# Two cross-attention layers on one core: image scores of layer 2 read from the row maxima's scores, and another order inside its slots

## The chip, the core and the metric

The kernel runs on one core of a Trainium2 chip. The metric is the device time of one execution in microseconds (us). A core has five engines that run side by side, each with its own order of instructions: TensorE (PE in the profile; PEld is its loading of weights, which overlaps the matmuls), VectorE (DVE), ScalarE (ACT), GpSimd (POOL) and SyncE (SP), which here only issues DMAs. ScalarE issues a few DMAs too. They wait for each other through semaphores.

## The reference

Sixteen sequences of 256 rows and 320 channels go through two cross-attention layers with 20 heads of 16. Each has a context of 256 tokens of 512 numbers, the last four of which are image tokens. Layer 2 is (cut to what matters):

```python
text_ehs = encoder_hidden_states[:, :-NUM_TOKENS]
ip_ehs = encoder_hidden_states[:, -NUM_TOKENS:]
q = heads(hidden_states @ W_q)
k_t, v_t = heads(text_ehs @ W_k), heads(text_ehs @ W_v)
probs_t = softmax(einsum('bhsd,bhtd->bhst', q, k_t) * attn_scale)
text_out = einsum('bhst,bhtd->bhsd', probs_t, v_t)
k_ip, v_ip = heads(ip_ehs @ W_k_ip), heads(ip_ehs @ W_v_ip)
attn_scores = einsum('bhsd,bhnd->bhsn', q, k_ip) * attn_scale
qsem = l2norm(einsum('bhst,bte->bhse', probs_t, text_ehs))
sem = einsum('bhse,bne->bhsn', qsem, l2norm(ip_ehs))
probs_ip = softmax(attn_scores + SEM_SCALE * sem) * spatial_mask
ip_out = einsum('bhsn,bhnd->bhsd', probs_ip, v_ip)
out = (text_out + ip_out) @ W_out + b_out + residual
```

`attn_scores`, the **image scores**, are 4 numbers per row and head. The **norm** of `qsem` is worked out as a square root of a form in the probabilities, not from `qsem` itself. Layer 1 differs in its semantic term and is not touched but at its last step.

## The kernel before

The work is cut into **slots**. A slot is one group of 4 heads of one batch: 16 batches of 5 groups make 80 slots a layer (NS = 80, NG = 5). Slots k = 0 to 79 are layer 1 (`slot0`), k = 80 to 159 are layer 2 (`slot1`); one or two more finish the pipeline. TensorE's order is written out by hand and pinned; in the main loop the other engines' orders are made by a scheduler. Between the parts of a slot stand points (0.33, 0.67, 1.0) at which `fill` runs every prepared step that is due by then: projections, keys, values, images, each a generator in `tasks` with due times counted in slots (L1046ff).

A layer-2 slot k has these parts. The 256 columns of a product are two halves (0 and 1).

- **T**, the scores with text rows on the partitions (L798), and **exps** of them on ScalarE (L811), which give `P[k]`. T reads rows XROW to KS1 of the stacked queries, which hold the row maxima. They are matmuls of 50 rows, two at a time in the array.
- **S**, the scores of group k+2 with query rows on the partitions (L803, 48 rows). VectorE reduces them to row maxima (L804) over the text columns [:T1]; columns T1 to S are those of the four image tokens.
- **attend1**: for group k-2 the values (L848), 32-column matmuls of `P`, and the ones' product `zone` (L851) over `W`; settled by VectorE and POOL (`settle1`: transpose L893, POOL copy L894, reciprocal L896, product L897).
- **rounded1** for group k: ScalarE rounds half of P (L829), POOL takes P minus that (L830), which gives `R` and `W`.
- **norm1** for group k-1: full 128-row matmuls of R (L839), four for n = 0 and three for n = 1, for both halves u of the group; VectorE multiplies them into `W` (L840). In the text, norm00, norm01, norm10 and norm11 are norm1(k-1, u, n).
- **maxima1** for group k+2: two small matmuls turn the maxima (L817), ScalarE copies them (L819) and issues two DMAs into rows of the stacked queries (L821).
- **stacks1** for group k+4: SyncE loads queries and keys (L648).

`both1(k, t)` issues T, S, the reduce, then what stands `between` (attend1), then the exps. The order is both1(k, 0) with attend1 between, norm00, fill 0.33, norm01, both1(k, 1), rounded 0, stacks, norm10, fill 0.67, norm11, rounded 1, maxima(k+2), fill 1.0.

Image work: `open1` projects the queries (`queries`), makes `kb` of the image keys with `image1` (two VectorE products of 128x384 with a constant mask, L529), multiplies it with the queries in nine matmuls (`prod`, L205) and transposes the product to `si` (L978). `image_softmax` (L904 to L946) takes the norms' parts `norms[b]` (`nt`, six numbers per row, head: index 0 the sum, 1 to 4 the semantic products, 5 the squared form), and `si`; `close1` multiplies with the image values (L954), projects and stores.

Other lines that the prediction names: L147 and L148 split context and keys into two parts (a cast on ScalarE, a difference on VectorE or POOL); L476 makes `tph`, a scaled copy of the context, on ScalarE; L541 is a difference of a split; L551 projects queries and output; L421 is a copy in the preparation. PSUM has banks for T, P (attend), X (all else) and S (BANKS).

Of the kernel before, what the change touches and what calls it, by code (L numbers as in the profile page):

```python
# [16 lines left out]
B = 16  # L17
S = 256
# [30 lines left out]
def xattn2(  # L49
# [47 lines left out]
    words, slots = {"ctb": 1024, "cta": 1024, "raw": 512, "rawc": 512, "kb": 1152, "si": 256, "sp": 128, "wC": 2 * 4 * (H * D + NIP), "mt": S, "mx": 2, "kst": 4 * S, "rs": 2 * S, "P": 4 * S}, {}  # L97
# [189 lines left out]
    kmask = const_tile([128, 3, 32], "kmask")  # L287
# [83 lines left out]
    def weights1():  # L371
# [3 lines left out]
        dma(cipn, cip_d)  # L375
        yield
# [33 lines left out]
    def weights6():  # L410
# [15 lines left out]
        dma(kmask, kmask_d.rearrange("(m p) c -> p m c", p=128))  # L426
# [97 lines left out]

    def image1(b):

        kb = buf("kb", [128, 2, 3, 32, NIP], FR)
        for s in range(2):
            nc.vector.tensor_mul(  # L529
                kb[:, s],  # L530
                f(kip[:, s, :, 4 * b : 4 * b + 4]).unsqueeze(2).to_broadcast([128, 3, 32, NIP]),
                kmask.unsqueeze(3).to_broadcast([128, 3, 32, NIP]),
            )
        return kb.rearrange("p s m c n -> p s m (c n)")
# [116 lines left out]
    def stacks1(k):  # L651
# [5 lines left out]
        qd = get("o1", b)[0]  # L657
# [126 lines left out]
    def both1(k, t, between=None):  # L784
# [7 lines left out]
        if c:  # L792
            st = [bank("T").rearrange("p (h t) -> p h t", h=2) for u in range(2)]
            lo = (0, DUP)[t]
            for j in range(2):
                for u in range(2):
                    rows = slice(64 * u, 64 * u + KS1)
                    mm(st[u][:, j], c[1][rows, j, lo : lo + 128], c[0][rows, j], start=True, stop=True)  # L798
        if a:
            for j in range(2):  # L800
                for u in range(2):
                    rows = slice(64 * u, 64 * u + XROW)
                    mm(sp[:, 2 * u + j], a[0][rows, j, t * 128 : (t + 1) * 128], a[1][rows, j], start=True, stop=True)  # L803
            anchor(nc.vector.tensor_reduce(maxes[k + 2][:, t], sp[:, :, :T1], axis=AX.X, op=ALU.max))  # L804
        if between:
            between()
# [35 lines left out]
    def attend1(k):  # L842
        b, g = divmod(k - NS, NG)
        v, pv = get("t1", b)[0], bank("P")
        for n in range(2):
            for s in range(4):
                h = V1W * (4 * g + s)
                mm(pv[32 * s : 32 * s + 32, :S], v[:, n, h : h + 32], P[k, s % 2][:, n, s // 2], start=n == 0, stop=False)  # L848
        for n in range(2):
            for s in range(4):  # L850
# [357 lines left out]
```

## Time and profile before

| | |
|---|---|
| median of 3 runs | 1620.4 us (1616.49 to 1623.62) |
| the profiled execution | 1612.52 us |
| its span in the profile | 1610.7 us, mean granted clock 0.977 |
| TensorE busy, of the span | 1518.9 us, 94%, 13194 matmuls |
| VectorE busy | 1212.2 us, 75% |
| ScalarE busy | 847.1 us, 53% |
| GpSimd busy | 1195.7 us, 74% |

The views answer: the page gives each engine's busy time and forty slices of the span (digits are tenths; PEclk is the clock that TensorE was granted). The windows give the same by stretches of 100 us. The groups give, by line and engine, count, busy time, mean duration in ns and the idle time just before with what ended it. The timeline gives single instructions, or runs of like ones, with their start. A matmul's duration contains the pipeline's tail, so the next one starts earlier than it ends.

### The profile page before, as it was taken

The numbers are of one execution on the slowest core, as the hardware profiler recorded it, in microseconds if no ns is written. First come the engines' busy times: TensorE is split into PE (matmuls) and PEld (weight loads), VectorE is DVE, ScalarE is ACT, GpSimd is POOL, SyncE is SP. The second block draws the span as 40 slices with busy tenths as digits, with TensorE's granted clock in tenths as the row PEclk, the third lists the DMA queues.
The fourth block names the chain that finished last, engine by engine and source line by source line (L and its number), as shares of the span: only waits on it lengthen the run. The fifth ranks groups of instructions, "written<-read, shape, count | busy, mean of one in ns | idle before, by whom it ended". The sixth has DMA issues, their size and how long they took to land.

```text
span 1610.7 us, 36262 instructions
## 1 busy us (share of the span) xinstructions
PE 1518.9 (94%) x13194; PEld 1218.1 (76%) x13194; DVE 1212.2 (75%) x2426; ACT 847.1 (53%) x1861; POOL 1195.7 (74%) x1227
## 2 busy tenths in 40 slices
PE   7899999999999899789999999999999999999996
PEld 6787878787878787577777777777777777777765
DVE  5466777777777678877877787778777887788785
ACT  5344545555555545446656556555655655565562
POOL 3358787878787867777688768876877787778785
PEclk9899999999999899799999999999999999999998
DMA  6767777777677576665424333433343333423301
GB/s 218 214 200 204 206 204 206 205 205 211 199 204 210 170 213 174 162 198 177 149 67 133 114 127 96 131 119 120 96 136 121 107 109 127 130 90 104 110 27 45
DMA packets 235741, 243.05 MB, mean 151 GB/s; under 512 B 19050, under 2 KB 219468, under 8 KB 235564
## 3 DMA queue, kind: packets, MB, share of 16 engines
q1 hardware_dynamic: 233356, 239.44, 49.7%
q8 instruction: 105, 1.72, 0.4%
q10 hardware_dynamic: 2208, 1.30, 0.3%
q14 instruction: 72, 0.59, 0.1%
HBM read 116.78 MB, written 88.18 MB: 127 GB/s over the span
## 4 chain that ended last, share of the span: by engine, by line
PE 63%; DMA 9%; DVE 8%; POOL 8%; ACT 4%; issue 3%; SPq 1%; ACTq 0%; POOLq 0%; DVEq 0%
PE X L205 16%; PE X L839 13%; PE X L551 7%; PE P L732 6%; PE P L848 4%; PE S L675 4%; PE T L798 3%; PE P L851 3%; PE T L699 3%; POOL wt L830 2%; DMA kd<-kst 2%; DMA qs<-qd 2%; DMA qs<-mt 2%; PE S L803 2%; DVE wt L840 1%
## 5 line engine op out<-in xcount | busy, mean ns | idle before, releaser
L705 POOL TENSOR_TENSOR P<-P,rs 128x512 f32<-128x512 f32 x320 | 413.8, 1313 | 149.6 <-ACT P L702 149.5
L830 POOL TENSOR_TENSOR wt<-P,ctb 128x512 f32<-128x512 f32 x320 | 419.0, 1324 | 95.0 <-ACT ctb L829 93.6
L839 PE MATMUL X<-ctb,gm 128*128 128x512 f32 x1120 | 329.9, 412 | 0.7 <-DVE wt L840 0.4
L702 ACT ACTIVATE P<-T 128x512 f32<-128x512 f32 x320 | 176.0, 595 | 211.8 <-PE T L699 113.9
L839 PEld LDWEIGHTS X<-ctb,gm 128*128 128x128 f32 x1120 | 188.9, 188 | 69.2 <-issue 15.2
L840 DVE TENSOR_TENSOR wt<-X,wt 128x512 f32<-128x512 f32 x320 | 218.4, 683 | 18.9 <-PE X L839 13.4
L804 DVE TENSOR_REDUCE mn<-S 128x4 fp32r<-128x1008 f32 x160 | 191.7, 1198 | 49.1 <-PE S L803 48.9
L829 ACT ACTIVATE ctb<-P 128x512 fp32r<-128x512 f32 x320 | 195.1, 630 | 40.1 <-PE X L839 35.8
L811 ACT ACTIVATE P<-T 128x512 f32<-128x512 f32 x320 | 173.1, 593 | 68.9 <-PE P L848 53.8
L677 DVE TENSOR_REDUCE mn<-S 128x4 fp32r<-128x716 f32 x160 | 142.5, 891 | 0.0
L699 PE MATMUL T<-qs,ks 127*128 127x256 f32 x640 | 111.7, 294 | 21.9 <-DVE tmp L749 9.8
L732 PE MATMUL P<-P,vr 128*32 128x256 f32 x1920 | 128.7, 404 | 0.9 <-DVE mx L604 0.9
L675 PE MATMUL S<-ks,qs 125*128 125x256 f32 x640 | 118.4, 309 | 4.9 <-DVE mn L677 2.8
L675 PEld LDWEIGHTS S<-ks,qs 125*128 125x128 f32 x640 | 89.2, 196 | 41.3 <-issue 36.2
L551 PE MATMUL X<-ho,wF 128*128 128x256 f32 x768 | 113.2, 291 | 6.5 <-DVE ho L541 3.0
L551 PE MATMUL X<-hq,wE 128*128 128x256 f32 x768 | 109.7, 286 | 7.1 <-ACT hq L540 3.2
L917 POOL TENSOR_TENSOR r<-u,rs 128x40 f32<-128x40 f32 (+2 forms) x17 | 108.7, 6394 | 7.4 <-DVE u L914 7.2
L551 PEld LDWEIGHTS X<-ho,wF 128*128 128x128 f32 x768 | 103.7, 195 | 12.7 <-DVE ho L541 4.6
L699 PEld LDWEIGHTS T<-qs,ks 127*128 127x128 f32 x640 | 92.5, 197 | 27.2 <-DVE tmp L749 11.2
L551 PEld LDWEIGHTS X<-hq,wE 128*128 128x128 f32 x768 | 102.3, 193 | 11.3 <-ACT hq L540 3.7
L205 PE MATMUL X<-cta,wA 128*128 128x252 f32 (+1 forms) x720 | 101.1, 287 | 8.9 <-ACT wA L147 5.8
L205 PEld LDWEIGHTS X<-cta,wA 128*128 128x128 f32 x720 | 94.3, 193 | 15.1 <-ACT wA L147 6.1
(207 smaller groups left out, 2854.9 us busy)
## 6 DMA issues: line engine op xcount, KB each, us to landing
qd<-q SPq DMA_DIRECT2D x96, 384.0 KB
qs<-tph SPq DMA_DIRECT2D x64, 308.0 KB
kd<-kst SPq DMA_DIRECT2D x73, 256.0 KB
rawc<-in_cT_dram SPq DMA_DIRECT2D x60, 256.0 KB
qs<-qd SPq DMA_DIRECT2D x80, 192.0 KB
ks<-kd SPq DMA_DIRECT2D x80, 192.0 KB
ks<-kd SPq DMA_DIRECT2D x160, 96.0 KB
qs<-qd SPq DMA_DIRECT2D x160, 96.0 KB
```

Source lines behind the costliest of these rows:

```text
L205: last = mm(out, lhs(a, k), rhs(b, k), start=i == 0, stop=i == len(terms) - 1)
L551: mm(pp, w(s, k, slice(m * 128, (m + 1) * 128)), a[:, t], start=i == 0, stop=i == len(terms) - 1)
L675: mm(sp[:, h], Q[: XROW + T0, h, t * 128 : (t + 1) * 128], K[: XROW + T0, h], start=True, stop=True)
L699: mm(st[p][:, j], K[:KS0, 2 * p + j, t * 128 : (t + 1) * 128], Q[:KS0, 2 * p + j], start=True, stop=True)
L702: exp = anchor(nc.scalar.activation(pt, st[p], AF.Exp, scale=SCALE))
L705: anchor(nc.gpsimd.tensor_mul(pt, pt, rs[:, t : t + 1].to_broadcast([128, 2, S])))
L732: mm(pv[32 * s : 32 * s + 32, o : o + S], v[:, vt, h : h + 32], P[k, s // 2][:, t, s % 2], start=vt < 2, stop=vt != 1,)
L804: anchor(nc.vector.tensor_reduce(maxes[k + 2][:, t], sp[:, :, :T1], axis=AX.X, op=ALU.max))
L829: nc.scalar.activation(R[k, u][:, t], P[k, u][:, t], AF.Copy, scale=0.5)
L830: anchor(nc.gpsimd.tensor_sub(W[k, u][:, t], P[k, u][:, t], f(R[k, u][:, t])))
L839: mm(yp, gm[:, gb], R[k, u][:, kt], start=i == 0, stop=i == len(blocks[n]) - 1)
L840: nc.vector.tensor_mul(W[k, u][:, n], yp, W[k, u][:, n])
```

## The change

The scores S of group k+2 are complete for all 256 context tokens, the image tokens too. The change copies their last four columns out of PSUM (`image_scores`, one VectorE copy of 128x16 per half, ahead of the reduce) into `sq`. After the last group of a batch one DMA writes `sq` into DRAM and, 0.6 slots later, eight DMAs read it back in the layout of `si` (`image_out`; 128 rows of 80 bytes each). `image1`, its mask `kmask`, the nine image matmuls and the transpose in `open1` go. The mask `bmask` of the image values is loaded through DRAM into the freed buffer.

The order in a layer-2 slot becomes: S, T (half 0), attend1(k-1), which is now the values of group k-1 and the ones' product of group k-2, T, S (half 1), maxima(k+1), norm00, fill 0.33, norm01, rounded 0, stacks, norm10, fill 0.67, norm11, rounded 1, fill 1.0. So the values come one group earlier, maxima one group later, and T and S of the two halves stand with attend1 alone between them. As the ones' product of a group's last number comes with the next group's values, the squared form (index 5) of a group stands one index further on in `norms`, with one more POOL copy a batch; layer 2's `gather` comes a slot earlier, and one step of `close1` is due at 10 instead of 9.67.

```diff
@@ -94,7 +94,7 @@
-    words, slots = {"ctb": 1024, "cta": 1024, "raw": 512, "rawc": 512, "kb": 1152, "si": 256, "sp": 128, "wC": 2 * 4 * (H * D + NIP), "mt": S, "mx": 2, "kst": 4 * S, "rs": 2 * S, "P": 4 * S}, {}
+    words, slots = {"ctb": 1024, "cta": 1024, "raw": 512, "rawc": 512, "kb": 1152, "si": 256, "sp": 128, "wC": 2 * 4 * (H * D + NIP), "mt": S, "mx": 2, "tmp": (NG + 1) * 48, "kst": 4 * S, "rs": 2 * S, "P": 4 * S}, {}
@@ -284,7 +284,6 @@
     kip = const_tile([128, 2, 3, BI], "kip", FR)
-    kmask = const_tile([128, 3, 32], "kmask")
@@ -373,6 +372,8 @@
         dma(cipn, cip_d)
+        hop = w1["hop"] = dram.tile([128, CP], F32, name="hop")
+        dma(hop, bmask_d)
         yield
@@ -423,7 +424,8 @@
         w1["ind"] = ind1
-        dma(kmask, kmask_d.rearrange("(m p) c -> p m c", p=128))
+        w1["bmask"] = f(buf("kb", [128, CP], FR, name="bmask"))
+        dma(w1["bmask"], w1["hop"])
         dma(vipd, vip)
@@ -522,17 +524,6 @@
-    def image1(b):
-
-        kb = buf("kb", [128, 2, 3, 32, NIP], FR)
-        for s in range(2):
-            nc.vector.tensor_mul(
-                kb[:, s],
-                f(kip[:, s, :, 4 * b : 4 * b + 4]).unsqueeze(2).to_broadcast([128, 3, 32, NIP]),
-                kmask.unsqueeze(3).to_broadcast([128, 3, 32, NIP]),
-            )
-        return kb.rearrange("p s m c n -> p s m (c n)")
-
     def split(src, neg, eng, tag):
@@ -654,7 +645,7 @@
         get("k1", b)
-        qd = get("o1", b)[0]
+        qd = get("o1", b)
         for u in range(2):
@@ -781,7 +772,28 @@
-    def both1(k, t, between=None):
+    image = {}
+
+    def image_scores(k, t, sp):
+
+        b, g = divmod(k - NS, NG)
+        if (g, t) == (0, 0):
+            image[b] = buf("sq", [128, 2, 4, NG * NIP], bufs=2)
+        sq = image[b]
+        nc.vector.tensor_copy(sq[:, t, :, NIP * g : NIP * (g + 1)], sp[:, :, T1:S])
+        if (g, t) == (NG - 1, 1):
+            sd = dram.tile([128, 2, 4, NG * NIP], F32, tag="sd", name="sd", bufs=2)
+            dma(sd, sq)
+            later(0.6, lambda: image_out(b, sd))
+
+    def image_out(b, sd):
+
+        si = image[b] = buf("si", [128, 8, NG * NIP], bufs=3)
+        for s in range(4):
+            for u in range(2):
+                dma(si[32 * s : 32 * s + 32, 4 * u : 4 * u + 4], sd[:, u, 2 * (s % 2) + s // 2].rearrange("(a r) x -> r a x", r=32))
+
+    def both1(k, t):
@@ -789,21 +801,26 @@
             sp = scores()
-        if c:
-            st = [bank("T").rearrange("p (h t) -> p h t", h=2) for u in range(2)]
-            lo = (0, DUP)[t]
+        def turned():
             for j in range(2):
...
                     mm(st[u][:, j], c[1][rows, j, lo : lo + 128], c[0][rows, j], start=True, stop=True)
-        if a:
+
+        def plain():
             for j in range(2):
...
                     mm(sp[:, 2 * u + j], a[0][rows, j, t * 128 : (t + 1) * 128], a[1][rows, j], start=True, stop=True)
+            image_scores(k + 2, t, sp)
             anchor(nc.vector.tensor_reduce(maxes[k + 2][:, t], sp[:, :, :T1], axis=AX.X, op=ALU.max))
-        if between:
-            between()
+
+        if c:
+            st = [bank("T").rearrange("p (h t) -> p h t", h=2) for u in range(2)]
+            lo = (0, DUP)[t]
+        for wanted, make in ((a, plain), (c, turned))[:: 1 if t == 0 else -1]:
+            if wanted:
+                make()
         if c:
@@ -840,31 +857,39 @@
     def attend1(k):
-        b, g = divmod(k - NS, NG)
-        v, pv = get("t1", b)[0], bank("P")
-        for n in range(2):
-            for s in range(4):
-                h = V1W * (4 * g + s)
-                mm(pv[32 * s : 32 * s + 32, :S], v[:, n, h : h + 32], P[k, s % 2][:, n, s // 2], start=n == 0, stop=False)
-        for n in range(2):
-            for s in range(4):
-                mm(pv[32 * s : 32 * s + 32, :S], zone, W[k, s % 2][:, n, s // 2], start=False, stop=n == 1)
-        settle1(b, g, pv)
+        pv = bank("P")
+        ours, before = k < 2 * NS, k > NS
+        if ours:
+            b, g = divmod(k - NS, NG)
+            v = get("t1", b)[0]
+            for n in range(2):
+                for s in range(4):
+                    h = V1W * (4 * g + s)
+                    mm(
+                        pv[32 * s : 32 * s + 32, :S],
+                        v[:, n, h : h + 32],
+                        P[k, s % 2][:, n, s // 2],
+                        start=n == 0,
+                        stop=n == 1 and not before,
+                    )
+        if before:
+            for n in range(2):
+                for s in range(4):
+                    mm(pv[32 * s : 32 * s + 32, :S], zone, W[k - 1, s % 2][:, n, s // 2], start=n == 0 and not ours, stop=n == 1)
+        settle1(k, pv)
...
         mine = k < 2 * NS
-        if k == NS:
-            yield lambda: maxima(k + 1)
-        elif k == NS + 1:
-            yield lambda: attend0(k - 2)
-        yield lambda: both1(k, 0, (lambda: attend1(k - 2)) if k > NS + 1 else None)
+        yield lambda: both1(k, 0)
+        yield lambda: (attend0 if k == NS else attend1)(k - 1)
+        yield lambda: both1(k, 1)
+        yield lambda: maxima(k + 1)
         if last:
...
             yield lambda: norm1(last, 0, 1)
-        yield lambda: both1(k, 1)
         if mine:
@@ -875,23 +900,24 @@
             yield lambda: rounded1(k, 1)
-        yield lambda: maxima(k + 2)
         yield 1.0
...
-    def settle1(b, g, pv):
+    def settle1(k, pv):
         hn = hsn
+        b, g = divmod(k - NS, NG)
+        if "na" not in w1:
+            w1["na"] = buf("nt", [128, 2, 8, 32], bufs=2, name="na")
+        na = w1["na"][:, (k - NS) % 2]
+        nc.vector.transpose(na.rearrange("p f c -> p (f c)"), pv[:, :S])
+        if g == 0 and b:
+            nc.gpsimd.tensor_copy(norms[b - 1][:, NG, :, 5], na[:, :, 21])
+        if b == B:
+            return
         if g == 0:
-            norms[b] = buf("tmp", [128, NG, 8, 6], bufs=2, name="n1")
-        nt = norms[b]
-        if "na" not in w1:
-            w1["na"], masks = [buf("nt", [128, 2, 8, 32], bufs=2, name="na") for i in range(2)]
-            w1["bmask"] = masks.rearrange("p a f c -> p (a f c)")[:, :CP]
-            dma(w1["bmask"], bmask_d)
-        na = w1["na"][:, (NG * b + g) % 2]
-        nc.vector.transpose(na.rearrange("p f c -> p (f c)"), pv[:, :S])
-        nc.gpsimd.tensor_copy(nt[:, g], na[:, :, 16:22])
+            norms[b] = buf("tmp", [128, NG + 1, 8, 6], bufs=2, name="n1")
+        nc.gpsimd.tensor_copy(norms[b][:, g], na[:, :, 16:22])
         rz = pv[:, S : S + 8]
@@ -904,14 +930,15 @@
         gs, n = slice(lo, hi), hi - lo
-        nt, si = norms[b][:, gs], get("o1", b)[1]
+        nt, si = norms[b][:, gs], image[b]
+        square = norms[b][:, lo + 1 : hi + 1, :, 5]
         pool = nc.gpsimd
...
         yield
-        nc.vector.scalar_tensor_tensor(u, u, EPS2 / 4, nt[:, :, :, 5], op0=ALU.mult, op1=ALU.max)
+        nc.vector.scalar_tensor_tensor(u, u, EPS2 / 4, square, op0=ALU.mult, op1=ALU.max)
         yield
@@ -970,14 +997,7 @@
-        kb = image1(b)
-        yield
-        sp = bank()[:, :S]
-        prod(sp, lambda s, k: kb[:, s, k], lambda s, k: qh[:, s, k], 3)
-        si = buf("si", [128, 8, 32], bufs=3)
-        nc.vector.transpose(si.rearrange("p f c -> p (f c)"), sp)
-        yield
-        return qd, si
+        return qd
@@ -1048,7 +1068,7 @@
         task(("i1", b), shifted(n, 6.67, 6.67, 6.67, 7.33, 7.33, 7.67, 7.67, 8, 8.33), lambda b=b: image_softmax(b, NG - 1 if b == B - 1 else 0), ("gathered", 1, b), ("taken", B + b - 1), *([("i1a",)] if b == B - 1 else []))
-        task(("c1", b), shifted(n + (1.67 if b > B - 3 else 0), 8.67, 8.67, 8.67, 8.67, 9, 9.67, 11.67, 13), lambda b=b: close1(b), ("i1", b), ("w4", 1))
+        task(("c1", b), shifted(n + (1.67 if b > B - 3 else 0), 8.67, 8.67, 8.67, 8.67, 9, 10, 11.67, 13), lambda b=b: close1(b), ("i1", b), ("w4", 1))
     task(("i1a",), [2 * NS + 0.1], lambda: image_softmax(B - 1, 0, NG - 1), ("i1", B - 2))
```

## The prediction

> **What bounds the kernel now.** I read the page's engine line and its slices first, then 100 us windows of layer 2, then TensorE's timeline.
>
> ```profile
> PE 1518.9 (94%) x13194; PEld 1218.1 (76%) x13194; DVE 1212.2 (75%) x2426; ACT 847.1 (53%) x1861; POOL 1195.7 (74%) x1227
> ...
> PE   7899999999999899789999999999999999999996
> ...
> PEclk9899999999999899799999999999999999999998
> ```
>
> ```profile
> 1000.00:1100.00 100.00, 98.62 (x841) 75.71 (x841) 77.95 (x146) 55.57 (x120) 76.00 (x81) 1.00 0.37 118
> 1100.00:1200.00 100.00, 99.04 (x858) 76.26 (x860) 79.05 (x145) 56.67 (x121) 75.63 (x78) 1.00 0.36 113
> ```
>
> The columns of the windows are length, then PE, PEld, DVE, ACT, POOL, clock, DMA share, GB/s. In layer 2 PE is busy 99% at the full clock and VectorE 78 to 79%, so a microsecond taken out of PE's order comes out of the span as long as no wait moves in. The rows of one stretch of PE, from the end of one slot into the second half of the next, are the prices I use (start, duration with the pipeline's tail; I go by differences of starts):
>
> ```profile
> 1121.00 0.86 PE L839 MATMUL X<-ctb,gm 128*128 128x512 f32 x3
> 1121.70 0.28 PE L817 MATMUL X<-ident_r,mn 128*4 128x128 f32 x2
> 1121.82 1.29 PE L205 MATMUL X<-q,kb 128*128 128x256 f32 x9
> 1123.03 0.51 PE L798 MATMUL T<-qs,ks 50*128 50x256 f32 x4
> 1123.37 0.41 PE L803 MATMUL S<-ks,qs 48*128 48x256 f32 x4
> 1123.71 1.07 PE L848 MATMUL P<-P,v1t 128*32 128x256 f32 x16
> 1124.60 1.05 PE L851 MATMUL P<-wt,zone 128*32 128x256 f32 x16
> 1125.57 1.20 PE L839 MATMUL X<-ctb,gm 128*128 128x512 f32 x4
> 1126.61 1.95 PE L205 MATMUL X<-wC,cta 128*128 128x324 f32 x12
> 1128.39 0.86 PE L839 MATMUL X<-ctb,gm 128*128 128x512 f32 x3
> 1129.18 0.51 PE L798 MATMUL T<-qs,ks 50*128 50x256 f32 x4
> 1129.53 0.40 PE L803 MATMUL S<-ks,qs 48*128 48x256 f32 x4
> 1129.86 1.20 PE L839 MATMUL X<-ctb,gm 128*128 128x512 f32 x4
> 1130.89 1.12 PE L551 MATMUL X<-ho,wF 128*128 128x256 f32 x8
> ```
>
> **1. The image matmuls go.** Once a batch, nine of them stand between 1121.82 and the T of the next slot at 1123.03, 1.21 us. Part of it is the step from full matmuls to the row-tiled T, which stays: three norm matmuls take 0.70 ahead of another full matmul (1121.00 to 1121.70) and 0.79 ahead of T (1128.39 to 1129.18), so 0.09. That leaves 1.1 a batch, x16 = **-17.5 us**. It cannot hide, since PE does not idle there.
>
> **2. A slot's order changes shape less often.** Before: full to T/S, S to the 32-column values and zone, zone to norm, norm01 to T/S again, S to norm10: five changes. After: full to S/T, T to values, zone to T/S, S to maxima: four. Gone are zone to norm (zone takes 0.97 where the equally long values take 0.89, so 0.08; the four norms after it take 1.04 against 4 x 0.233 = 0.93, so 0.11) and norm01 to T (0.09): together 0.28. New is zone to T, for which there is no row. Its cheap end is S to values, 0.34 as T to S is 0.34, that is nil; its dear end is 0.28, the whole saving. I take 0.07, near the rows of one such edge (0.08 and 0.09): -0.21 a slot, x80 = **-17 us** (bounds 0 to -22).
>
> The Trainium skill, TensorEngine Tiling (Array Packing), section Tiling Modes, Key Properties, says that a change of tiling mode drains TensorE. The edges of 0.08 to 0.11 us above agree; the S to values edge, at nil, does not show it.
>
> **3. VectorE's exchange.**
>
> ```profile
> L529 DVE TENSOR_TENSOR kb<-kip,kmask 128x384 fp32r<-128x384 f32 x32 | 35.6, 1115 | 5.9 <-PE X L205 5.9
> ...
> L978 DVE STREAM_TRANSPOSE si<-X 128x256 f32<-128x256 f32 x16 | 7.0, 437 | 0.5 <-PE X L205 0.5
> ...
> L804 DVE TENSOR_REDUCE mn<-S 128x4 fp32r<-128x1008 f32 x160 | 191.7, 1198 | 49.1 <-PE S L803 48.9
> L811 ACT ACTIVATE P<-T 128x512 f32<-128x512 f32 x320 | 173.1, 593 | 68.9 <-PE P L848 53.8
> ...
> L896 DVE RECIPROCAL P<-nt 128x8 f32<-128x8 f32 x80 | 16.5, 207 | 2.2
> L421 DVE COPY rawc<-X 64x128 f32<-64x128 f32 x3 | 0.8, 269 | 0.5 <-PE X L205 0.5
> ```
>
> Gone a batch: 2 x 1.115 + 0.437 = 2.67 us. New: ten copies of 128x16 out of PSUM. The nearest rows are a 128x8 reciprocal, 0.207, and a 64x128 copy from PSUM, 0.269; I take 0.2, so 2.0 a batch. VectorE loses 0.7 us of about 43 (79% of a 54 us batch): nothing on PE by itself. One more POOL copy of eight columns a batch, one DMA of the scores out and eight back, the mask's extra hop: costed at nothing: the last scores of a batch come two slots after its first (they are made two slots ahead of their group), the softmax that reads them is due 6.67 slots after, so over four slots of about 10.9 us lie between. If that cover goes, the softmax starts later, and what is late next is the image product.
>
> **4. The new waits inside a slot.** From the starts above, the new slot is S 0, T 0.34, values 0.68, zone 1.57, T of half 1 at 2.5, S of half 1 at 2.85. T's banks of half 0 are free after the two exps, 0.34 + 0.51 + 2 x 0.59 = 2.0: 0.5 us of slack if ScalarE is free. It should be: most of its idle time before L811 (53.8 of 68.9) is for values of the slot before last, which the new order runs one slot earlier. The S bank of half 0 is free after copy and reduce, 0.4 + 0.2 + 1.2 = 1.8: 1.0 us of slack, if VectorE is free. Price at nothing; gone, it is PE's wait one for one. Values of k-1 use exps of the slot before, zone the products of two slots before: both done.
>
> **5. The row maxima come a slot later than they did.** This is the wait I charge for. The old program made them at the end of slot k-2 for T of slot k; the new one makes them in slot k-1, after S of half 1, and T of slot k waits for two small DMAs from ScalarE's queue. The rows below are the first T of a batch, a stall in its first slot, the T of the second slot, and the first T of the next batch, 54.4 us later. In the built order of the first slot of a batch, ScalarE runs: exps, two casts L147, maxima copy, first DMA, q cast, one rounding, two tph (which wait for POOL's L148), second DMA.
>
> ```profile
> 1090.56 0.50 PE L798 MATMUL T<-qs,ks 50*128 50x256 f32 x4
> ...
> 1099.03 0.70 PE L954 MATMUL X<-rs,rs 128*128 128x256 f32 x2 [0.42 <-DVE wt L840]
> ...
> 1100.47 0.50 PE L798 MATMUL T<-qs,ks 50*128 50x256 f32 x4
> ...
> 1144.92 0.51 PE L798 MATMUL T<-qs,ks 50*128 50x256 f32 x4
> ```
>
> ```profile
> 1089.89 0.34 ACT L819 CAST mt<-X 4x256 fp32r<-4x256 f32 x1
> ...
> 1090.29 1.31 ACTq L821 DMA_DIRECT2D qs<-mt  x2
> ...
> 1095.47 0.72 ACT L476 ACTIVATE tph<-cta 128x252 fp32r<-128x252 f32 x2 [1.97 <-POOL cta L148]
> 1096.10 0.35 ACT L559 CAST q<-X 128x256 fp32r<-128x256 f32 x1
> 1096.35 0.63 ACT L829 ACTIVATE ctb<-P 128x512 fp32r<-128x512 f32 x1
> ...
> 1097.84 0.62 ACT L147 CAST cta<-rawc 128x512 fp32r<-128x512 f32 x1
> ```
>
> Exps of half 1 end at 2.5 + 0.5 + 1.2 = 4.2; two casts 5.4; maxima copy 5.8; first DMA 6.4; q 6.8; rounding 7.4; tph 8.1: the second DMA is issued then. How long it takes is read from the rows of ScalarE's DMA queue (packets, MB, share) in narrow windows. Of two DMAs issued from 1133.77 the last packet falls into 1136.0 to 1136.5, first row of that queue below; of two issued from 1122.93, into 1127.0 to 1127.5, second row:
>
> ```profile
> 1122.93 1.58 ACTq L821 DMA_DIRECT2D qs<-mt  x2
> ...
> 1133.77 1.31 ACTq L821 DMA_DIRECT2D qs<-mt  x2
> ```
>
> ```profile
> q10 hardware_dynamic: 1, 0.00, 0.1%
> ```
>
> ```profile
> q10 hardware_dynamic: 1, 0.00, 0.1%
> ```
>
> With 0.65 for the first issue, that is 1.6 to 2.1 and 3.4 to 3.9 us from the second issue's start. So it lands 9.7 to 12.0 after the slot's start. The slot is 9.91 now (1090.56 to 1100.47, its 0.42 of stall in it), less 0.21; T stands 0.34 later in the next one: 10.0. The added stall is between nothing and 2.0; I take 0.9, a little below the middle, since the issue at 8.1 assumes that ScalarE is never ahead of my chain. x16 = **+14 us**. In the other four slots no such work stands before the second DMA, or the slot is longer by up to 2 us.
>
> **The sum.** -17.5 - 17 + 14 = -20.5 us. The profiled execution took 1612.52 (span 1610.7): 1592 on its own scale. It lies 8 us below the median of the runs, 1620.4, on which the forecast is **1600**. Its own range, with the maxima's wait from 0 to 2.0 and the saved edges from 0.28 to 0.1 a slot: 1580 to 1616. A difference below 0.5% (8 us) is no change by these runs' spread (1616.49 to 1623.62).
>
> **Rivals.**
> *Whole gain, waits vanish.* No wait for the DMA, the new edge nil, and the stall that PE has now (0.42) gone as well: -17.5 - 22 - 7 = -46, 1574. For: ScalarE no longer waits for L848, VectorE loses its 2.2 us block of L529. Against: the tph order above. 0.12.
> *Nothing.* Zone to T costs as much as the edges removed, and the maxima's wait eats 1.1 us a batch: about 1620. For: no row shows column tiles followed by row tiles. 0.13.
> *Slower: the maxima's DMA late in most slots.* Its place is ScalarE's queue between the maxima's copy and the next T. It decides from 2.15 us of added wait a batch (1.1 + 5 x 0.21). If three of five slots lose 1.2 us (landing at the dear end), it is 3.6 - 2.15 = +1.45 a batch, +23: 1643. For: a landing of 3.4 to 3.9 us where the slot leaves about 5 from the maxima to the next T. Against: ScalarE is just 56% busy. 0.2.
> That the change does not remove what it says is not open: the nine matmuls are not in the built order.
>
> **Numbers.** Forecast 0.55, whole gain 0.12, nothing 0.13, slower 0.2. Of the forecast's 0.55, 0.03 ends within 0.5% and 0.02 beyond. Faster by over 0.5%: 0.12 + 0.5 = 0.62; within: 0.13 + 0.03 = 0.16; slower: 0.2 + 0.02 = 0.22. The range is 1574 to 1632: it leaves out most of the slower rival (0.15) and what lies beyond the whole gain (0.05).
>
> **What would show it.** PE's group of q,kb gone and its busy time 30 us or more smaller; from norm01 no step to T; the start of T after zone at 0.9 to 1.0 (right) or above 1.1 (edge dear); PE or PEld waiting at T for DMA qs<-mt in the first slot of each batch only (right), in most slots (slower rival), in none (whole gain); ScalarE's idle time at the exps no longer put down to values. The forecast is wrong if PE waits for the S bank (VectorE's reduce or copy), which I price at nothing, or if the batch period of 54.3 us does not fall to about 53.

## The result and the profile after

| | before | changed kernel |
|---|---|---|
| median | 1618.7 us (4 runs, 1616.49 to 1623.62) | 1559.79 us (4 runs, 1559.22 to 1561.12) |
| profiled execution | 1612.52 us | 1559.42 us |
| its span | 1610.7 us | 1557.6 us |

The ratio is 0.9639, with a 95% interval of 0.9622 to 0.9657: 59 us faster, where 20 were forecast and the range ended at 1574. The direction was right; the gain forecast was about a third of the measured one.

From the page of the changed kernel, the engine line and two of the slice lines:

```profile
PE 1476.3 (95%) x13050; PEld 1205.6 (77%) x13050; DVE 1173.8 (75%) x2539; ACT 845.6 (54%) x1861; POOL 1195.0 (77%) x1243
...
PE   7899999999999989878999999999999999999996
...
PEclk9899999999999999899999999999999999999998
```

From its windows, in the middle of layer 2 (columns as before the change):

```profile
1000.00:1100.00 100.00, 100.00 (x899) 79.40 (x898) 80.25 (x172) 61.51 (x132) 82.11 (x91) 1.00 0.41 127
1100.00:1200.00 100.00, 100.00 (x899) 79.44 (x898) 79.68 (x172) 61.27 (x132) 82.16 (x91) 1.00 0.42 129
```

PE went from 98.6 and 99.0% to no gap, at the same clock. That is one per cent, and the layer-2 batch became 7% shorter. Part of the rest is matmuls and changes of shape that went; the other part is waits, of which less than half showed as idle time before (0.66 us a batch of 1.44, below), since a matmul's duration contains its pipeline's tail and covers a short wait. All of it shows in the starts. The timeline of PE over the first slot of a batch and the beginning of the second:

```profile
1065.36 0.50 PE L814 MATMUL S<-ks,qs 48*128 48x256 f32 x4
1065.70 0.40 PE L808 MATMUL T<-qs,ks 50*128 50x256 f32 x4
1066.03 1.07 PE L868 MATMUL P<-P,v1t 128*32 128x256 f32 x16
1066.92 1.05 PE L878 MATMUL P<-wt,zone 128*32 128x256 f32 x16
1067.89 0.51 PE L808 MATMUL T<-qs,ks 50*128 50x256 f32 x4
1068.24 0.40 PE L814 MATMUL S<-ks,qs 48*128 48x256 f32 x4
1068.57 0.29 PE L834 MATMUL X<-ident_r,mn 128*4 128x128 f32 x2
1068.69 1.14 PE L856 MATMUL X<-ctb,gm 128*128 128x512 f32 x4
1069.67 1.12 PE L542 MATMUL X<-hq,wE 128*128 128x256 f32 x8
1070.62 1.77 PE L856 MATMUL X<-ctb,gm 128*128 128x512 f32 x7
1072.23 1.46 PE L981 MATMUL X<-rs,rs 128*128 128x256 f32 x6
1073.33 1.05 PE L856 MATMUL X<-ctb,gm 128*128 128x512 f32 x3
1074.31 0.50 PE L814 MATMUL S<-ks,qs 48*128 48x256 f32 x4
1074.65 0.40 PE L808 MATMUL T<-qs,ks 50*128 50x256 f32 x4
```

The slot is 8.95 us, of 9.91 before. S of half 1 stands 2.88 after S of half 0, as worked out (2.85). norm01 and norm10 now run as seven matmuls in 1.61 us, 0.23 each, with no edge between them, and the six image-value matmuls (L981; L954 before) run without the wait of 0.42.

To add this up, take each run of like matmuls and measure from its start to the start of the next run, over ten batches in the middle of layer 2, from the profiled execution. Microseconds a batch:

| | before | changed | difference |
|---|---|---|---|
| image product | 1.21 | 0 | -1.21 |
| norms | 18.01 | 16.89 | -1.12 |
| maxima's matmuls | 0.94 | 0.61 | -0.33 |
| S, T, values, zone | 16.04 | 16.08 | +0.04 |
| image values | 1.79 | 1.11 | -0.68 |
| output projection | 3.25 | 2.93 | -0.32 |
| all else (queries, keys, values) | 13.10 | 12.90 | -0.20 |
| batch period | 54.34 | 50.52 | -3.82 |

Three parts come out: the image product, 1.21; the shape edges, 1.17 (norms, S, T, values, zone, and 0.09 of the maxima, for the edge from them to T); and waits that ended, 1.44 (0.24 of the maxima, image values, projection, the rest). The forecast held the first two and not the third. As idle time of PE, the profile before has 0.66 us a batch there, the profile after 0.04.

Sixteen times 3.82 would be 61; the profiled executions differ by 53. Measured at the ones' product of equal groups, the changed kernel is 5.3 us ahead at the sixth group of layer 2 and 54.5 at the 71st, 3.8 a batch; from the 77th (56.3) to the last it gives 4.7 back. These slots have little work beside the chain of a group, and there the wait shows that the forecast had charged to every batch:

```profile
1512.28 0.29 PE L834 MATMUL X<-ident_r,mn 128*4 128x128 f32 x2
1512.40 3.48 PE L856 MATMUL X<-ctb,gm 128*128 128x512 f32 x14
1515.88 0.35 PE L808 MATMUL T<-qs,ks 50*128 50x256 f32 x1
1517.89 0.47 PE L808 MATMUL T<-qs,ks 50*128 50x256 f32 x3 [1.66 <-DMA qs<-mt]
```

T waits for the maxima's DMA until 5.6 us after the maxima's matmuls. The clock has a part in it too: from 1518.9 to 1522.3 us TensorE was granted half of it (0.66 on average from 1518 to 1523), which the kernel before did not have in its last slots until 1593.7.

### The profile page after: what moved, and what is told of

Same layout as the page of the kernel before. It is cut to its first block, busy times and chain, and to the rows that moved or that the text cites. A ratio compares the mean times of both kernels' runs of the same rounds, so it can differ in the third digit from the quotient of the medians.

```text
span 1557.6 us, 36272 instructions
## 1 busy us (share of the span) xinstructions
PE 1476.3 (95%) x13050; PEld 1205.6 (77%) x13050; DVE 1173.8 (75%) x2539; ACT 845.6 (54%) x1861; POOL 1195.0 (77%) x1243
## 4 chain that ended last, share of the span: by engine, by line
PE 76%; DMA 9%; DVE 5%; POOL 3%; ACT 2%; issue 2%; SPq 1%; ACTq 0%; POOLq 0%; DVEq 0%
PE X L856 16%; PE X L205 16%; PE X L542 9%; PE P L723 6%; PE P L868 5%; PE P L878 4%; PE S L666 4%; PE T L808 3%; PE T L690 3%; PE S L814 3%; DMA qs<-mt 2%; DMA kd<-kst 2%; PE X L504 2%; DMA qs<-qd 2%; PE X L981 1%
## 5 line engine op out<-in xcount | busy, mean ns | idle before, releaser
L847 POOL TENSOR_TENSOR wt<-P,ctb 128x512 f32<-128x512 f32 x320 | 410.3, 1303 | 81.7 <-ACT ctb L846 81.6
L856 PE MATMUL X<-ctb,gm 128*128 128x512 f32 x1120 | 303.9, 401 | 0.3 <-DVE wt L857 0.3
L857 DVE TENSOR_TENSOR wt<-X,wt 128x512 f32<-128x512 f32 x320 | 214.4, 679 | 25.1 <-PE X L856 20.3
L856 PEld LDWEIGHTS X<-ctb,gm 128*128 128x128 f32 x1120 | 196.3, 189 | 31.3 <-issue 0.6
L846 ACT ACTIVATE ctb<-P 128x512 fp32r<-128x512 f32 x320 | 187.9, 627 | 19.0 <-PE X L856 14.8
L723 PE MATMUL P<-P,vr 128*32 128x256 f32 x1920 | 132.0, 409 | 3.8 <-DVE mx L595 1.9
```

What stands on the lines that cost most here:

```text
L723: mm(pv[32 * s : 32 * s + 32, o : o + S], v[:, vt, h : h + 32], P[k, s // 2][:, t, s % 2], start=vt < 2, stop=vt != 1,)
L846: nc.scalar.activation(R[k, u][:, t], P[k, u][:, t], AF.Copy, scale=0.5)
L847: anchor(nc.gpsimd.tensor_sub(W[k, u][:, t], P[k, u][:, t], f(R[k, u][:, t])))
L856: mm(yp, gm[:, gb], R[k, u][:, kt], start=i == 0, stop=i == len(blocks[n]) - 1)
L857: nc.vector.tensor_mul(W[k, u][:, n], yp, W[k, u][:, n])
```

## The experiments

Question one: which part of the change ended the waits? Each half was run alone.

**The order alone.** The kernel before, with the new slot order and what belongs to it (the shifted index, the due time of 10); image product, mask and transpose stay.

```diff
-        yield lambda: both1(k, 0, (lambda: attend1(k - 2)) if k > NS + 1 else None)
+        yield lambda: both1(k, 0)
+        yield lambda: (attend0 if k == NS else attend1)(k - 1)
+        yield lambda: both1(k, 1)
+        yield lambda: maxima(k + 1)
...
-        yield lambda: both1(k, 1)
...
-        yield lambda: maxima(k + 2)
```

> The kernel before with the new slot order alone; image product, its mask and its transpose stay as they were. The batch period fell from 54.34 to 50.52 us with both parts. Theory 'order': the waits of TensorE in the old order came from the order (the reduce of half 1 stood on VectorE just ahead of the norm products), so with the order alone they vanish too: period 50.52 + 1.21 (image product) = 51.7, about 1577 to 1580 us. Rival 'relief': they vanish because VectorE lost 2.67 us a batch of image work, so they stay here (1.4 us a batch): period 53.1, about 1600 us.

Measured: 1608.54 us, ratio to before 0.9951 (0.9932 to 0.9969), period 53.63. Both theories were too hopeful. The waits at the image values did end (1.11 a batch, as in the changed kernel), but others came: T of half 1 to S of half 1 takes 1.0 us a batch more, the projections about 0.7 (output 3.37, where the kernel before has 3.25 and the changed one 2.93). The timeline of VectorE, then of PE, in the slot that follows an image product:

```profile
1018.97 1.11 DVE L529 TENSOR_TENSOR kb<-kip,kmask 128x384 fp32r<-128x384 f32 x1 [0.23 <-PE X L205]
1020.00 0.44 DVE L994 STREAM_TRANSPOSE si<-X 128x256 f32<-128x256 f32 x1
1020.37 1.27 DVE L529 TENSOR_TENSOR kb<-kip,kmask 128x384 fp32r<-128x384 f32 x1
1021.56 1.19 DVE L803 TENSOR_REDUCE mn<-S 128x4 fp32r<-128x1008 f32 x1
```

```profile
1018.97 0.50 PE L802 MATMUL S<-ks,qs 48*128 48x256 f32 x4
...
1021.51 0.51 PE L796 MATMUL T<-qs,ks 50*128 50x256 f32 x4
1022.80 0.51 PE L802 MATMUL S<-ks,qs 48*128 48x256 f32 x4 [0.79 <-DVE mn L803]
```

As soon as the image product has freed `kb`, VectorE makes it for the next batch: 2.6 us with the transpose, just when S of half 0 is ready. The reduce starts 2.6 us after S of half 0, and S of half 1, due after 2.9, waits until the reduce is over. In the kernel before, the same block stood at the same place (there the reduce started at 1125.40, 2.0 after S), but S of half 1 came over six microseconds after S of half 0, at 1129.53, and PE did not wait for the reduce:

```profile
1124.21 1.27 DVE L529 TENSOR_TENSOR kb<-kip,kmask 128x384 fp32r<-128x384 f32 x1
1125.40 1.20 DVE L804 TENSOR_REDUCE mn<-S 128x4 fp32r<-128x1008 f32 x1
```

The other waits of the run with the order alone are for VectorE too by its view of waits: at the transposes behind the output projection for `gm` (3.4 us in ten batches), at the norms for `wt` (0.9 us).

**The image scores alone.** The kernel before, with the copies and DMAs and without image product, mask and transpose.

```diff
+            image_scores(k + 2, t, sp)
             anchor(nc.vector.tensor_reduce(maxes[k + 2][:, t], sp[:, :, :T1], axis=AX.X, op=ALU.max))
...
-        kb = image1(b)
...
-        prod(sp, lambda s, k: kb[:, s, k], lambda s, k: qh[:, s, k], 3)
```

> The kernel before with the image scores from the row maxima's scores alone; the slot order stays the old one. Theory 'order': only the image product's 1.21 us a batch goes, the old waits stay: period 53.1, about 1600 us. Rival 'relief': the waits of 1.4 us a batch go too: period 51.7, about 1578 us. A third: the copies and the small DMAs add waits of their own: above 1605 us.

Measured: 1598.68 us, ratio 0.9893 (0.9862 to 0.9923), period 53.65: the time is that of the theory 'order' (1600), the period is not (53.1), so the agreement in time is partly luck. The image product goes and the old waits stay; the run of image values even grows from 1.79 to 2.18 us a batch. VectorE's timeline shows why: there the query difference stands ahead of norm01's product, not behind it, VectorE idles 0.13 us before it, and a copy (0.08) comes on top, so the reduce of half 1 and norm10's product behind it start 0.37 us later, counted from the image values. So the two halves give 0.71 and 0.69 us a batch alone and 3.82 together. Neither theory of mine had that: the order ends the old wait at the image values, but it pays only once VectorE's image block is gone, which otherwise makes new waits.

**Half 1 late.** The changed kernel with T and S of half 1 back between the norms.

```diff
-        yield lambda: both1(k, 1)
         yield lambda: maxima(k + 1)
...
         if last:
             yield lambda: norm1(last, 0, 1)
+        yield lambda: both1(k, 1)
```

> The changed kernel with T and S of half 1 put back between norm01 and the first rounding; the rest stays new. Shape edges: zone to full, full to row and row to full come back, by the sums of starts 0.22 us a slot, 1.1 a batch, +18 us. Theory 'order' adds the waits behind the late reduce, up to 1.4 a batch: 1585 to 1600 us. Rival 'relief': edges alone: 1577 us.

Measured: 1585.04 us, ratio 0.9796 (0.9757 to 0.9836), period 52.47, 1.95 more than the changed kernel. The norms take 17.89 instead of 16.89: 0.2 us a slot for the edges, as the forecast had it. The wait at the image values comes back (1.65 a batch), and that behind the output projection (3.37). Its view of waits names the cause (us in total, times, longest from 920 to 1450 us):

```profile
PE X L981 <- DVE wt L857: 2.8, 10, 0.3
```

and the kernel before shows it on VectorE's timeline:

```profile
1097.19 1.19 DVE L804 TENSOR_REDUCE mn<-S 128x4 fp32r<-128x1008 f32 x1
1098.30 0.67 DVE L840 TENSOR_TENSOR wt<-X,wt 128x512 f32<-128x512 f32 x1
1098.90 1.29 DVE L955 TENSOR_TENSOR hT<-hT,X 128x256 f32<-128x256 f32 x3
```

The late reduce (1.19 us) stands on VectorE just ahead of norm10's product L840, which frees the bank that the next image value needs; PE resumed at 1099.03, when L840 was done. With both reduces at the front of the slot, VectorE meets norm10's product with no reduce ahead of it.

**The due time of the projection.** The changed kernel with the step at 9.67 again.

```diff
-        task(("c1", b), shifted(n + (1.67 if b > B - 3 else 0), 8.67, 8.67, 8.67, 8.67, 9, 10, 11.67, 13), lambda b=b: close1(b), ("i1", b), ("w4", 1))
+        task(("c1", b), shifted(n + (1.67 if b > B - 3 else 0), 8.67, 8.67, 8.67, 8.67, 9, 9.67, 11.67, 13), lambda b=b: close1(b), ("i1", b), ("w4", 1))
```

> The changed kernel with the output projection's step of close1 due at 9.67 slots again instead of 10. If that due time removed the old wait of 0.32 us a batch ahead of the projection (split ho late), it comes back: +5 us, 1565. If the slot order removed it: no change, 1558 to 1562.

Measured: 1559.17 us (1555.8 to 1564.67), as the changed kernel; the projection takes 2.87 us a batch. So the due time did not remove that wait. The order alone did not either (3.37, with the due time of 10), nor the image scores alone (3.25), nor the order with half 1 late (3.37): it takes the whole order without VectorE's block. The wait is also not where I had put it, ahead of the projection, but behind it: PE waits at the small transposes `X<-ident,sp` for VectorE's `gm` (1.8 us in ten batches of the kernel before).

Question two: is it VectorE's block between S of half 0 and its reduce?

**A dead block.** The changed kernel with two products of 128x384 whose result nobody reads.

```diff
         qh, qd = yield from queries(1, xs)
+        dead = buf("dead", [128, 3, 32, NIP], mybir.dt.bfloat16)
+        for s in range(2):
+            nc.vector.tensor_mul(
+                dead,
+                f(kip[:, s, :, 4 * b : 4 * b + 4]).unsqueeze(2).to_broadcast([128, 3, 32, NIP]),
+                w1["bmask"].rearrange("p (m c n) -> p m c n", m=3, n=NIP),
+            )
```

> The changed kernel with two VectorE products of 128x384 a batch, as before at the old place in open1, whose result nobody reads; no image matmuls. The kernel with the order alone lost 1.0 us a batch between T and S of half 1 (waiting for the reduce of half 0) and about 0.7 ahead of the projections. Theory 'block': VectorE's block of 2.2 us between S of half 0 and its reduce is what costs it: those 1.7 us a batch come back, +27, about 1587 us, with PE waiting at S for the reduce. Rival 'product': the nine matmuls and the PSUM bank that they hold cost it: no change, 1558 to 1564.

Measured: 1579.17 us, but this run answers nothing. The products depend on nothing late, so the scheduler ran all 32 before layer 2 began, from 647.5 to 705.4 us in the profile:

```profile
L1001 DVE TENSOR_TENSOR dead<-kip,kb x32: 515/558/1520, 647.5 to 705.4; 128x384 bf16<-128x384 f32 x32
```

The loss, 21.6 us, is all there ahead of layer 2's first group (the granted clock up to 750 us was lower too, 0.94 against 0.96); the period is 50.56, that of the changed kernel. So whether the nine matmuls and their bank add something of their own stays untested. Work has to depend on the moment at which it is to stand, so the next two runs repeat the reduce itself.

**The reduce three times, half 0 or half 1.** In the slot of one group of each batch, the same maxima made again into the same place; the other run has t == 1.

```diff
-            anchor(nc.vector.tensor_reduce(maxes[k + 2][:, t], sp[:, :, :T1], axis=AX.X, op=ALU.max))
+            again = 2 if t == 0 and (k + 2 - NS) % NG == 3 else 0
+            for i in range(1 + again):
+                anchor(nc.vector.tensor_reduce(maxes[k + 2][:, t], sp[:, :, :T1], axis=AX.X, op=ALU.max))
```

> The changed kernel with the reduce of half 0 done three times instead of once in one slot of each batch (that of group 3), output the same: 2.4 us more on VectorE between S of half 0 and S of half 1. Theory 'S bank': in that slot the copy starts 0.76 us after S, the last reduce ends at 0.84 + 3 x 1.2 to 4.9 (a transpose falls in between), S of half 1 stands 2.87 after S: PE waits 1.6 to 2.0 there once a batch, +26 to +32, about 1588 us. Rival 'load': VectorE has room (80% busy) and the halves are decoupled: no change, 1558 to 1564.

> The same 2.4 us of VectorE work in the same slot, but on half 1. Theory 'S bank': the bank is wanted again only by the next slot, over 5 us later; the norm products come up to 2.4 us later, of which PE sees little: 1558 to 1570. Rival 'load': if VectorE's total is what counts, it loses as much as the run with half 0.

Measured: 1608.71 us with half 0 (ratio 0.9939, 0.9918 to 0.9959), 1577.75 with half 1 (0.9742, 0.9723 to 0.9761). VectorE and PE with half 0:

```profile
1013.69 0.16 DVE L783 COPY sq<-S 128x16 f32<-128x16 f32 x1
1013.77 2.44 DVE L818 TENSOR_REDUCE mn<-S 128x4 fp32r<-128x1008 f32 x2
1016.13 0.44 DVE L915 STREAM_TRANSPOSE nt<-P 128x256 f32<-128x256 f32 x1
1016.49 1.17 DVE L818 TENSOR_REDUCE mn<-S 128x4 fp32r<-128x1008 f32 x1
```

```profile
1017.80 0.51 PE L814 MATMUL S<-ks,qs 48*128 48x256 f32 x4 [1.83 <-DVE P L924]
```

S of half 1 waits for the last reduce; from T to S the batch takes 2.0 us more, the upper end of what was expected. (The releaser is named L924, a reciprocal that ended with the reduce.) The period is 53.91, 3.4 more than the changed kernel's, and the other 1.4 are the clock. In most batches of this run TensorE was granted half the clock for 3.4 us soon after that wait, and the matmuls that stand there (values' projection, norms) take longer. Two batches of it, one without such a stretch and one with it (the column before the last two is the granted clock):

```profile
922.70:975.40 52.70, 50.88 (x461) 40.39 (x455) 42.36 (x89) 30.99 (x67) 40.02 (x44) 1.00 0.39 123
975.40:1029.40 54.00, 52.16 (x459) 41.54 (x455) 42.86 (x89) 30.89 (x67) 42.98 (x48) 0.97 0.38 121
```

Batches at full clock take 52.5 to 52.7, 1.9 to 2.2 more than the changed kernel's: 31 to 35 us in all, at the upper end of the forecast or just above it. The other 16 or so of the 49 us fit eleven such stretches in layer 2 at 1.4 each (an estimate). The same work on half 1 costs 1.2 us a batch at full clock and nothing between T and S (0.34 as ever): it delays products, and those keep PE waiting at norms, at a query projection and at the next S. So the place of VectorE's work decides what it costs, about 2.1 or 1.2 us a batch, and with the longer wait came the clock's 1.4; that the work is free behind S of half 1 was too much said.

Question three: what of the values one group earlier, and of the maxima?

**Values and ones' product of one group.** Two runs of the changed kernel with the old grouping, group k-2 for both. In the first, the exps of group k stand ahead of the values of k-2 in the program, and as the two groups share P's buffers the values are worked out from the newer group's exps; its output is another one and only its waits are of use.

```diff
-        yield lambda: (attend0 if k == NS else attend1)(k - 1)
+        if k == NS:
+            yield lambda: attend0(k - 1)
+        elif k > NS + 1:
+            yield lambda: attend1(k - 2)
```

> The changed kernel with attend1 of one group again: values and ones' product of group k-2 both, in the new place between the halves. Theory: the exps of half 0 wait for P's buffers until the values of k-2 are done (about 1.6 us after the slot's start), so T's banks come free at about 3.0 and T of half 1, due at 2.5, waits 0.5 us a slot: 2.4 a batch, +38, about 1598 us, PE waiting at T for the exps. Rival: P's buffers are free earlier and only the order of T and S counts: 1558 to 1564.

Measured: 1671.78 us (ratio 1.0323, 1.0285 to 1.0362). PE waits at the values for the exps of the same slot:

```profile
PE P L865 <- ACT P L828: 33.7, 42, 1.3
```

That answers another question than the one asked: values that need exps of their own slot cost 1.4 us a slot (the period is 57.7), of which 0.8 shows as idle time. The second run puts the exps behind the values, as before the change:

```diff
-        yield lambda: both1(k, 0)
+        yield lambda: both1(k, 0, (lambda: attend1(k - 2)) if k > NS + 1 else (lambda: attend0(k - 1)) if k == NS else None)
```

> The changed kernel with values and ones' product both of group k-2 between the halves, and the exps of half 0 behind them in program order (P has four buffers, two a group, so they have to wait for the values of k-2). Theory: exps start at about 1.7 us of the slot and end at 2.9, T of half 1, due at 2.5, waits 0.5 us a slot: 2.4 a batch, +38, about 1598 us; PE waits at T for the exps in most slots. Rival: T's banks are free in time, and only T and S standing together counts: 1558 to 1564.

Measured: 1573.63 us (ratio 0.9723, 0.9698 to 0.9748), period 51.45. The exps do wait for the values, as they did before the change and no longer do in the changed kernel; the groups of the two kernels, this one first:

```profile
L830 ACT ACTIVATE P<-T 128x512 f32<-128x512 f32 x320 | 172.4, 595 | 95.4 <-PE P L867 51.6 <-PE T L808 43.7
```

```profile
L828 ACT ACTIVATE P<-T 128x512 f32<-128x512 f32 x320 | 173.4, 594 | 103.7 <-PE T L808 101.9
```

But PE does not wait at T, where I had put the price (38 us): T to S and zone to T are unchanged. It loses 0.9 a batch further down, behind the maxima (0.35), at the output projection (0.32), T to values (0.14) and the norms (0.11). So taking the values a group earlier is worth about 14 us of the 59, and not by T's banks. That it is by exps that come sooner fits the lines above but is not shown: at the norms PE waits for exps seven times and for VectorE's product four times (920 to 1400 us).

**The maxima later.** The changed kernel with `maxima(k + 1)` behind norm00, or, in the other run, behind norm01.

```diff
         yield lambda: both1(k, 1)
-        yield lambda: maxima(k + 1)
         if last:
             yield lambda: norm1(last, 0, 0)
+        yield lambda: maxima(k + 1)
```

> The changed kernel with the maxima one norm (0.98 us) later. In the last slots T waited for the maxima's DMA until 5.6 us after their matmuls. From matmuls to T the five slots of a batch have 8.4, 6.8, 6.1, 8.5 and 6.25 us. Theory 'near the edge': with 1 us less two slots fall short by 0.5 and 0.35: 0.85 a batch, +14, about 1573 us. Rival 'wide margin': the path is about 3.5 us where the queue is not at the end: no change, 1558 to 1564.

> The changed kernel with the maxima behind norm01, 2.6 to 3.5 us later than now, by slot. Theory 'near the edge' (5.6 us from matmuls to landing): the gaps shrink to 4.9, 4.2, 3.5, 5.4 and 3.15, waits of 6.9 us in all a batch, +110, about 1670 us. Rival 'wide margin' (3.5 us): only the last slot falls short, by 0.35: +6, about 1566 us.

Measured: 1567.45 us (ratio 0.9689, 0.9659 to 0.9718) and 1607.22 (0.9939, 0.9915 to 0.9962); periods 51.25 and 53.42. Both lie between the theories. By slots of a batch, from the maxima's matmuls to T (median of ten batches), and what T then waited beyond its usual 0.33 (mean). A row is the slot in which the maxima stand; their T is at the head of the next slot:

| slot of the batch | changed: gap, wait | behind norm00: gap, wait | behind norm01: gap, wait |
|---|---|---|---|
| first (S at 1065.36) | 6.1, 0.04 | 5.2, 0.3 | 3.5, 0.6 |
| second | 8.55, 0 | 7.6, 0 | 5.5, 0 |
| third | 6.2, 0 | 5.3, 0 | 3.2, 0.7 |
| fourth | 8.4, 0 | 7.6, 0 | 4.95, 0.7 |
| fifth | 6.8, 0 | 5.85, 0 | 4.8, 0 |

In the changed kernel one batch in ten waits 0.4 us in its first slot, none elsewhere. One microsecond later it is three in ten (0.7, 1.1 and 1.3), in that slot alone; behind norm01 it is three slots of five in nearly every batch. From matmuls to landing it takes 3.9 us in the third slot of the last run, 4.1 in its first, up to 6.5 in its fourth, and 5.9 to 6.4 in the first slot of the batches that wait behind norm00: a path whose length varies by over 2 us, against a smallest gap of 6.1. So the forecast had the right slot for its wait, and the place at which the change stands is within a microsecond of it.

The maxima's DMA explains 0.3 of the 0.73 us by which the first period grew and 1.9 of the 2.9 of the second; the rest is mostly the norms' (0.3 and 0.5) and in the second the output projection's wait (0.4).

**The last slots.** The changed kernel with the maxima at the head of the last three slots.

```diff
+        early = k >= 2 * NS - 3
+        if early:
+            yield lambda: maxima(k + 1)
         yield lambda: both1(k, 0)
```

> The changed kernel with the maxima of the last three slots moved to the head of their slot, ahead of S. In the last slots, which have little else, T waited 1.66 us for the maxima's DMA; moved 3.2 us earlier they land in time. Theory: 1.7 us less and up to as much again from what follows, 1556 to 1558 us. Rival: the end is bound by the last batch's image softmax, so that it starts no earlier: 1559 to 1561.

Measured: 1558.77 us (1552.87 to 1562.18, 5 runs), not told apart from 1559.79. In its profile T waits no more in the last slots, and from the ones' product of group 76 to the last matmul it takes 48.1 us instead of 50.5. But these 2.4 us are not shown to come from the maxima: the dead block's run, with the last slots of the changed kernel and T's wait in them (1.8 us), takes 48.0 there, and the changed kernel's own profile had half the clock for 3.4 us of this stretch. So the wait ended, and nothing shows that the end came sooner for it, which fits the rival; that the last image softmax binds the end is not shown by this run.

## Why the prediction was right in direction and wrong in size

**Step 1, the image product: right.** 1.1 us a batch expected, 1.21 measured.

**Step 2, the edges: right.** 0.21 us a slot expected, 1.17 / 5 = 0.23 measured; 0.2 came back with half 1 late. The new edge from zone to T (0.98 from zone's start to T's, against 0.89 for the equal values) costs the 0.09 of the others, near the 0.07 taken. The Trainium skill's rule that a change of tiling mode drains TensorE (TensorEngine Tiling (Array Packing), Tiling Modes, Key Properties) fits that edge too, from column tiles to row tiles: 0.09.

**Step 3, VectorE's exchange: the copy was too dear, and the block was priced in the wrong order.** A copy is 0.16 us busy and, overlapped, moves the reduce by 0.08:

```profile
L783 DVE COPY sq<-S 128x16 f32<-128x16 f32 x160 | 25.9, 162 | 17.2 <-PE S L814 16.8 <-DMA qs<-qd 0.3
```

I put the removal of the 2.67 us block at "nothing on PE by itself". In the old order that is true (image alone: 53.65, just the product less and a bit of wait more). In the new order it is not: step 4 asked for VectorE to be free at the front of the slot, and the block stood just there. The two edits were costed one by one against the old kernel and added; the order alone shows what the second costs without the first.

**Step 4, the waits inside the slot: right for both edits together.** PE waits at S nowhere and at T only where step 5 has it, in one batch of ten. S's banks, with the 1.0 us of slack that I gave them, were indeed the tight point: with three reduces S of half 1 came 2.0 late.

**Step 5, the maxima's DMA: the wait charged at 0.9 a batch (+14 us) was not there.** My chain had the second DMA issued 8.1 us after the slot's start, behind a rounding and two tph. The profile of the changed kernel, ScalarE in that slot:

```profile
1069.40 1.14 ACT L147 CAST cta<-rawc 128x512 fp32r<-128x512 f32 x2
1070.43 0.35 ACT L836 CAST mt<-X 4x256 fp32r<-4x256 f32 x1
1070.82 0.63 ACTq L838 DMA_DIRECT2D qs<-mt  x1
1071.55 0.37 ACT L550 CAST q<-X 128x256 fp32r<-128x256 f32 x1 [0.76 <-PE X L856]
1071.72 0.63 ACTq L838 DMA_DIRECT2D qs<-mt  x1
1071.82 0.64 ACT L846 ACTIVATE ctb<-P 128x512 fp32r<-128x512 f32 x1
1072.35 0.70 ACT L478 ACTIVATE tph<-cta 128x252 fp32r<-128x252 f32 x2
```

The issue came at 1071.72, 6.4 after S at 1065.36, while the q cast ran and before the rounding and tph started. The last packets fall into the window 1073.5 to 1074.0,

```profile
q10 hardware_dynamic: 5, 0.00, 1.9%
```

and T ran unhindered at 1074.65, as in nine of ten batches. That the wait exists, and that this slot is next to it, the runs with later maxima show.

**The step that failed most is one that the sum did not have.** The prediction read the windows' 99% as PE without waits, counted one stall ("its 0.42 of stall in it") and let that stand, so the old order's waits entered its sum as nothing to be won. The waits that ended are 1.44 us a batch, 23 us. They were waits for VectorE: at the image values for the product behind the late reduce (0.68), at the transposes behind the projection for `gm` (0.32), and smaller ones. With the 14 of step 5 and 4 by which steps 1 and 2 were short, that is 41 us; 8 less, since sixteen times the period's 3.82 overstates the whole by so much, is 33, the miss on the scale of the profiled executions (53 against 20.5). The rival "whole gain" named the mechanism (no DMA wait, the stall gone) and priced it at 0.42 a batch, so even it ended at 1574. One sum of the prediction is added up wrong: with a wait of 2.0 and edges of 0.1 its own range ends at -17.5 - 8 + 32 = +6.5 us, 1627 and not 1616; the miss does not come from that.

## What to carry to other kernels

Where PE is 99% busy, measure from start to start of like runs before deciding that nothing waits: of 1.4 us of waits in a 54 us batch, 0.66 showed as idle time. Two edits that meet on one engine have no separate prices: the order was worth 0.7 us a batch with VectorE's image block, and 3.1 without it (3.82 less the 0.69 of the image part alone). Put an engine's long, early-needed work (the reduces) where nothing that frees a bank is queued behind it.

## What was not expected of the hardware

In the built order ScalarE's second DMA stands behind the rounding and two activations tph; the trace has it issued 0.1 us before the first and 0.6 before the second of them starts, once their semaphores were there (POOL's L148, that tph waits for, ended at 1071.4). It is so in all 13 such slots of layer 2. As far as this trace shows, a DMA on ScalarE's queue is not held by the execution of the instructions ahead of it; that their waits hold it fits the times, and no run takes the two apart.

In the run with half 0 reduced three times, PE waits 1.8 us at S once a batch, and 11 of the 14 such waits from 800 to 1510 us are followed, 0.4 to 1.8 us after their end, by 3.4 us at half the clock. The changed kernel's wait of 1.66 us in its last slots is followed by one 1.0 us later, the dead block's of 1.8 by none. The 11 waits of 1.3 us from 900 to 1480 us in the run whose values need exps of their own slot have none behind them. So a wait of under 2 us can cost more than its length; what decides whether the clock falls, no run settles.
